# Messages by natural edge tile, and the dispatch placed between the turns of the sums, in a two-layer GNN and mixture-of-experts kernel

## The chip, the cores and the metric

The kernel runs on one core of a Trainium2 chip. The metric is device microseconds of one execution, from the launch to the end on that core. Before the change three runs gave 4209.37, 4212.74 and 4214.22 us; their median, 4212.74 us, is the time before. The five engines are called by the names of the profile: PE (TensorE, with PEld for its weight loads), DVE (VectorE), ACT (ScalarE), POOL (GpSimd) and SP (SyncE, which issues transfers).

## The reference, cut to what matters

There are 6250 nodes of 256 features (49 blocks of 128 nodes), and 100,000 edges, sorted by `dst` and in random order of `src`. Layer 0 is a graph convolution and a mixture of experts, layer 1 a relational convolution and a second mixture:

```python
x = x + _L0_gnn_ref(_layernorm(x), edge_index, edge_weight, W, b, W1, b1, W2, b2)
x = x + _L0_ffn_ref(_layernorm(x)[None], router_w, w1, b1, w2, b2)[0]     # 8 experts, top 2
x = x + _L1_gnn_ref(edge_index, _layernorm(x), edge_type_8, weight, h_bias, loop_weight)
x = x + _L1_ffn_ref(_layernorm(x)[None], ...)[0]                           # 6 experts, top 2
```

The convolution of layer 0 is what the change touches. In it `row` is `src`, `col` is `dst`, and every node has a loop of weight 1:

```python
deg = segment_sum(ew_sl, row_sl)
norm = rsqrt(deg)[row_sl] * ew_sl * rsqrt(deg)[col_sl]
msgs = (h @ W)[col_sl] * norm[:, None]
h7 = segment_sum(msgs, row_sl) + b
out = relu(h7 @ W1 + b1) @ W2 + b2
```

So a row of `dst` is read for each edge, weighted, and summed at `src`. Then each node is normed, its two experts are chosen, and its row is sent to each of them.

## The kernel before, in words

**Keys (to 418 us).** The edges are written to a table in DRAM of 782 tiles of 128 edges (L152 to L189). A check finds whether they are sorted (L206), and a branch (L209) reorders them if not. `tile_list` (L243) then makes a list of tiles by block of `dst`: a tile whose edges lie in two blocks is in the list once for each, so the list has T = 830 entries, padded to TL = 832. The tiles are gathered in the list's order into `M` (L317). `dloc` is an edge's row within the entry's block; an edge of the other block is masked (`mine`, L335). `srcT`, `ewT`, `dlocT` and `idxT` are the transposed columns, one per entry (L352 to L355). From `srcT` come an edge's block by source and its row in it; `eq` (L547) holds 49 masks of 832 columns, from which are counted (`pcnt`, L555) and placed (`ppos`, L603 to L605) all edges in order of their source, and from which the degrees come (L665 to L680, DCH = 32 columns at a time). `at` (L614) is each message's place in `msgs`; a masked edge has the place NOWHERE, past the end.

**Messages (418 to 1505 us, L736 to L773).** `acc` holds the rows of all 49 blocks in SBUF, scaled by `dinv` (L731). For each list entry, one fp32 matmul of a 128x128 selection `sT` (L753, eight entries at a time, from `lane_rows`) with the entry's block of `acc` gives 128 rows (L758; the profile has two records for each such matmul). ACT weights them (L761), and POOL scatters them with one indirect DMA to their places in `msgs` (L764), which checks bounds, so that NOWHERE is skipped. Four buffers of eight entries (`msg`, L754) are in flight. X is loaded and `b2` added on the way (L743 to L751).

**Sums by source (1505 to 2003 us, L777 to L799).** The messages come back in order of source, eight tiles at a time, on SP's and ACT's queues in turn (L783, three buffers). DVE computes `key` (L785) and half of the selections `m` (L787), POOL the other half, each one ahead of its matmul (L795). PE multiplies (L797, into one of four PSUM buffers), and DVE adds to the tile's block of `acc` (L799). Which block that is is read from a register, so the address is known at run time only.

**Dispatch (2003 to 2206 us).** For 13 groups of four blocks, four stages run one behind the other (`in_stages`, L1063, L1071). `hidden0` scales `acc` on ACT (L974), transposes it, and applies Relu. `tokens` multiplies by W2 (L989), adds to X (L992) and takes the norm's statistics (L390 to L401). `choose` norms on ACT (L1003), multiplies with the router (L1009), and picks two experts (`route`, L851, on DVE but for an Exp). `send` counts places (L1028 to L1047) and issues two indirect DMAs per block (L1051). Then the counts of the experts are closed (L1078 to L1138) and the experts' tiles are fetched (L1156).

The weights of layer 0's experts (`fw1`, `fw2`, 2 MB each), their biases and W2 are loaded on SP's queue at the start of the dispatch (L930 to L934). What follows, the experts of layer 0, the products of layer 1 (`hx`), and its sums with layer 1's experts between their turns (`layer1`, L1395), is not changed but for where its memory lies.

**What sets the order.** [...] The framework orders instructions by their place in the program and by when it expects them to be ready, but it does not move one into or out of a branch. Reads and writes of `acc` at run-time addresses count as touching all of it.

Of the kernel before, what the change touches and what calls it, by code (L numbers as in the profile page):

```python
# [32 lines left out]
NOWHERE = 127 + 128 * 1024  # L33
TS = TL + NT
# [5 lines left out]
DCH = 32  # L40
# [12 lines left out]
def gnn_ffn_kernel(ctx: ExitStack, tc: tile.TileContext, a, out):  # L53
# [18 lines left out]
    g0p = graph0.enter_context(tc.tile_pool(name="graph0", bufs=1))  # L72
    loading = ctx.enter_context(ExitStack())
# [203 lines left out]

    turn_i = sp.tile([128, Q * 128], I32, name="turn_i")
    nc.gpsimd.iota(turn_i, pattern=[[1, Q * 128]], base=0, channel_multiplier=0)
    turn = g0p.tile([128, Q * 128], F32, name="turn")  # L280
# [43 lines left out]

    Mf = M.bitcast(F32)
    dloc = sp.tile([128, Q, 128], F32, name="dloc")
    srcm = sp.tile([128, Q, 128], F32, name="srcm")
    idxf = sp.tile([128, Q, 128], F32, name="idxf")
    mine = sp.tile([128, Q, 128], F32, name="mine")
    dlocb = sp.tile([128, Q, 128], BF16, name="dlocb")  # L330
# [3 lines left out]
    nc.scalar.copy(dlocb, dloc)  # L334
    nc.vector.tensor_scalar(mine, dloc, 0.0, None, op0=OP.is_ge)  # L335
    nc.vector.scalar_tensor_tensor(mine, dloc, 128.0, mine, op0=OP.is_lt, op1=OP.mult)
    nc.vector.scalar_tensor_tensor(srcm, M[:, :, :, 1], 1.0, mine, op0=OP.add, op1=OP.mult)
    lane_rows = dram.tile([Q * 128, 128], BF16, name="lane_rows")
    nc.sync.dma_start(lane_rows.rearrange("(q p) e -> p q e", p=128), dlocb)


    def to_edges(name, pool, rows, dt):
        t = pool.tile([128, Q * 128], dt, name=name)
        for q0 in range(0, Q, 4):
            n = min(4, Q - q0)
            pt = psum_mm(f"p_{name}{q0}")
            for q in range(n):
                nc.tensor.transpose(pt[:, q * 128 : (q + 1) * 128], rows(q0 + q), ident)
            nc.scalar.copy(t[:, q0 * 128 : (q0 + n) * 128], pt[:, : n * 128])
        return t  # L350

    srcT = to_edges("srcT", g0p, lambda q: srcm[:, q], F32)  # L352
    ewT = to_edges("ewT", g0p, lambda q: Mf[:, q, :, 2], F32)
    dlocT = to_edges("dlocT", ed, lambda q: dloc[:, q], BF16)
    idxT = to_edges("idxT", ed, lambda q: idxf[:, q], I32)  # L355
# [56 lines left out]
    def transpose_to(name, dest, x, bias=None):  # L412

        pt = p_tr.tile([128, 2, 128], F32, tag="tr", name=f"pt_{name}")
        for k in range(2):
            nc.tensor.transpose(pt[:, k, :], x[:, k * 128 : (k + 1) * 128], ident)  # L416
        if bias is None:
            nc.scalar.copy(dest, pt)
        else:
            for k in range(2):  # L420
                nc.scalar.activation(dest[:, k, :], pt[:, k, :], AF.Identity, bias=bias[k])
# [63 lines left out]
    mv0 = g0p.tile([128, NT, 2], F32, name="mv0")  # L485
# [6 lines left out]
    ve0 = g0p.tile([128, NT], F32, name="ve0")  # L492
    nc.vector.tensor_scalar(ve0, mv0[:, :, 1], EPS, None, op0=OP.add)
    rstd0 = rsqrt("ln0", ve0, [128, NT])
    shift0 = g0p.tile([128, NT], F32, name="shift0")
# [40 lines left out]
    srcT_i = kp.tile([128, TL], I32, name="srcT_i", tag="t1")  # L536
    nc.vector.tensor_scalar(srcT_i, srcT[:, :TL], -1.0, None, op0=OP.add)
    key_i = kp.tile([128, TL], I32, name="key_i", tag="t2")
    nc.vector.tensor_scalar(key_i, srcT_i, 7, None, op0=OP.arith_shift_right)
    hib = kp.tile([128, TL], BF16, name="hib")  # L540
    nc.vector.tensor_copy(hib, key_i)
    nc.vector.tensor_scalar(key_i, srcT_i, 127, None, op0=OP.bitwise_and)
    lob = kp.tile([128, TL], BF16, name="lob")
    nc.vector.tensor_copy(lob, key_i)
    eq = kp.tile([128, NT, TL], BF16, name="eq")
# [7 lines left out]
    for b in range(NT):  # L553
        for h in range(2):
            nc.tensor.matmul(  # L555
                pcnt[h][:NT, :TH],
                sel[:, NT - 1 - b : 2 * NT - 1 - b],
                eq[:, b, h * TH : (h + 1) * TH],
                start=(b == 0),
                stop=(b == NT - 1),  # L560
            )
    cnts = kp.tile([NT, TL], F32, name="cnts", tag="t1")
    for h in range(2):
        nc.scalar.copy(cnts[:, h * TH : (h + 1) * TH], pcnt[h][:NT, :TH])
    base = kp.tile([NT, TL], F32, name="base", tag="t3")
    one = ones[:NT, 0:1].to_broadcast([NT, TL])
    nc.vector.tensor_tensor_scan(base, one, cnts, 0.0, op0=OP.mult, op1=OP.add)
    tots = kp.tile([NT, 1], F32, name="tots")
    nc.vector.tensor_copy(tots, base[:, TL - 1 :])
# [12 lines left out]
    base_i = kp.tile([NT, TL], I32, name="base_i", tag="t2")  # L582
    nc.vector.scalar_tensor_tensor(base_i, base, start0, cnts, op0=OP.add, op1=OP.subtract)
    qr = kp.tile([64 + NT, TL], F16, name="qr")
    nc.vector.memset(qr, 0.0)
    half_i = kp.tile([NT, TL], I32, name="half_i", tag="t4")
# [10 lines left out]
    pos = kp.tile([128, TL], F32, name="pos", tag="t3")  # L597
    nc.vector.memset(pos, float(NOWHERE))
    for b in range(NT):
        for h in range(2):  # L600
            cs = slice(h * TH, (h + 1) * TH)
            pp = psum_mm(f"ppos{b}_{h}")
            nc.tensor.matmul(pp[:, :TH], beforeb, eq[:, b, cs], start=True, stop=False)  # L603
            nc.tensor.matmul(pp[:, :TH], selq[:, b : b + 1].to_broadcast([64 + NT, 128]), qr[:, cs], start=False, stop=True)
            nc.vector.copy_predicated(pos[:, cs], eq[:, b, cs].bitcast(U16), pp[:, :TH])  # L605
        next(xws, None)

    place = kp.tile([128, TL], I32, name="place", tag="t1")
    nc.vector.tensor_copy(place, pos)
    slot = kp.tile([128, TL], I32, name="slot", tag="t2")  # L610
    nc.vector.tensor_scalar(slot, place, 7, None, op0=OP.arith_shift_right)
    nc.vector.tensor_scalar(place, place, 127, None, op0=OP.bitwise_and)
    at = g0p.tile([128, TL], I32, name="at")
# [3 lines left out]
    past_s = kp.tile([NT, TL], F32, name="past_s", tag="t4")  # L617
# [8 lines left out]
    lasts = g0p.tile([1, 56], I32, name="lasts")  # L626
    nc.vector.memset(lasts, TS - 1)
    nc.vector.tensor_scalar(lasts[:, :NT], plast[:1, :NT], -1.0, None, op0=OP.add)
    for b0 in range(0, NT, 8):
        slots = blocks_of(lasts, b0, [ENG.SP], TS - 1)  # L630
        for b in range(min(8, NT - b0)):
            ins = nc.sync.dma_start(by_tile[:, bass.ds(slots[b], 1), :], none[:, 0:1, :])
            tc.declare_no_dep(ins.ins, group="tails", reason="every block has a last tile of its own")
            tc.add_to_no_dep_group("tails", ins.ins)
    blks = g0p.tile([1, TL], I32, name="blks")
    firsts = g0p.tile([128, TL], F32, name="firsts")
    first_of = g0p.tile([NT, 128], F32, name="first_of")
# [12 lines left out]
    parts = kp.tile([128, 3, TL], BF16, name="parts")  # L650
    rest = kp.tile([128, TL], F32, name="rest", tag="t1")
    nc.vector.tensor_copy(parts[:, 0], ewT[:, :TL])
    nc.vector.tensor_sub(rest, ewT[:, :TL], parts[:, 0])
# [8 lines left out]
    for c0 in range(0, TL, DCH):  # L662
# [16 lines left out]
        for c in range(DCH):  # L679
# [5 lines left out]
                stop=(c0 + c == TL - 1),  # L685
# [24 lines left out]
    expand = ctx.enter_context(ExitStack())  # L710
    xp = expand.enter_context(tc.tile_pool(name="expand", bufs=3))

    def lanes_of(t0):

        rows = xp.tile([128, 8, 128], BF16, name=f"rows{t0}", tag="rows")
        nc.sync.dma_start(
            rows,
            lane_rows[t0 : t0 + 8, :].rearrange("(o t) e -> o t e", o=1).to_broadcast([128, 8, 128]),
        )
        return rows  # L720

    ahead = [lanes_of(t0) for t0 in (0, 8, 16)]
# [11 lines left out]


    for t0 in range(0, TL, 8):  # L736
        blocks = blocks_of(blkd, t0, [ENG.PE], NT)
        n = min(8, T - t0)
        rows = ahead.pop(0)
        if t0 + 24 < TL:  # L740
            ahead.append(lanes_of(t0 + 24))

        if t0 % 80 == 40 and t0 // 80 < 4:  # L743
            t = t0 // 80 * 12
            nc.sync.dma_start(X[:, t : t + 12, :], xv[:, t : t + 12, :])
        if t0 == 400:
            nc.sync.dma_start(X[:last, NT - 1, :], a["x"][(NT - 1) * 128 :, :])
        if t0 >= 440 and t0 % 8 == 0 and (t0 - 440) // 8 * 2 < NT:
            t = (t0 - 440) // 8 * 2
            k = min(2, NT - t)  # L750
# [751 lines left out]
```

## Time and profile before

| | us |
|---|---|
| median of three runs (4209.37 to 4214.22) | 4212.74 |
| the profiled execution | 4220.04 |
| its span, first to last instruction | 4218.3 |
| PE busy, share of the span | 3288.1 (78%) |
| POOL busy | 2307.8 (55%) |
| DVE busy | 2072.4 (49%) |
| ACT busy | 1168.6 (28%) |

Around the span lie 1.7 us. The stages of the span are: keys 418, messages 1087, sums by source 498, dispatch 203, experts of layer 0 270, products of layer 1 479, layer 1's sums and experts 1263. In rows of groups, the first number after the bar is the group's busy time in us, the second the mean ns of one instruction; behind the next bar stands the engine's idle time just ahead of them, and what ended most of it. In rows of a timeline, the first two numbers are the start and the duration in us, and the brackets hold the idle time ahead of it and its releaser. "issue" as a releaser means that nothing in the profile was waited for.

### The profile page before, as it was taken

Reading aid. Unit: us, or ns where it says so; the run is one execution under the profiler, and the core shown is the slowest. Engines: PE = TensorE matmul, PEld = TensorE weight load, DVE = VectorE, ACT = ScalarE, POOL = GpSimd, SP = SyncE. Lnnn points to the kernel's source line nnn. Section 1 sums busy time; section 2 is a strip of 40 time slices with the busy share of each in tenths; the row PEclk is TensorE's granted clock in tenths of the full one; section 3 lists DMA queues with packets and bytes.
Section 4 is the critical chain, followed back from the end, with each engine's and each line's share of the span. In section 5 each row is a group of like instructions: output and inputs, shape, how many; then the busy total and the mean of one; then the engine's idle time right before and its main releaser. Section 6 shows DMA issues by size and latency. Waiting matters only on the chain.

```text
span 4218.3 us, 49934 instructions
## 1 busy us (share of the span) xinstructions
PE 3288.1 (78%) x13207; PEld 2125.4 (50%) x13207; DVE 2072.4 (49%) x5527; ACT 1168.6 (28%) x2569; POOL 2307.8 (55%) x2488
## 2 busy tenths in 40 slices
PE   2886555565555559999749977999679999999999
PEld 1565444444444335554537743444256666666656
DVE  5676200000000058888563357665456666666652
ACT  3312433333333300000434433665012222222213
POOL 1000777777777755555470048333767777777750
PEclk9998877767777779999769988999589999999999
DMA  4413433333333356666333335444655555555540
GB/s 169 155 43 110 153 124 121 123 123 120 121 122 122 108 190 230 225 227 209 106 115 107 109 105 201 194 194 205 190 142 151 152 151 153 150 155 150 146 117 9
DMA packets 235392, 611.60 MB, mean 145 GB/s; under 512 B 44269, under 2 KB 128482, under 8 KB 215139
## 3 DMA queue, kind: packets, MB, share of 16 engines
q0 software_dynamic: 102928, 294.81, 22.5%
q1 hardware_dynamic: 105200, 234.80, 16.6%
q10 hardware_dynamic: 26976, 78.69, 5.4%
q8 instruction: 115, 1.88, 0.2%
q14 instruction: 173, 1.42, 0.1%
HBM read 371.46 MB, written 243.18 MB: 146 GB/s over the span
## 4 chain that ended last, share of the span: by engine, by line
PE 42%; DVE 10%; POOL 4%; issue 3%; DMA 3%; ACT 2%; DVEq 1%; SPq 0%; POOLq 0%; ACTq 0%
PE ph_e1a L428 6%; PE py1a L904 6%; PE pa1a L823 5%; PE pa L797 5%; PE ph_e2a L428 5%; PE phx L1265 4%; DVE acc L799 3%; PE pf L1184 2%; PE pf L1200 2%; POOL m L795 2%; DVE rest L1275 1%; PE pg L989 1%; DVE acc L827 1%; PE pt_fh L416 1%; DVE hx L1259 1%
## 5 line engine op out<-in xcount | busy, mean ns | idle before, releaser
L764 POOL DMA_INDIRECT msgs<-msg,at x830 | 833.1, 1004 | 599.2 <-ACT msg L761 388.6
L815 POOL DMA_INDIRECT g1a<-hx,idxT x830 | 826.6, 996 | 321.1 <-PE pa1a L823 148.0
L758 PE MATMUL px<-acc,sT 128*128 x1660 | 601.4, 541 | 481.7 <-ACT msg L761 447.6
L758 PEld LDWEIGHTS px<-acc,sT 128*128 128x128 f32 x1660 | 459.3, 284 | 623.1 <-ACT msg L761 487.6
L761 ACT ACTIVATE msg<-px,ewT 128x256 f32<-128x256 f32 x830 | 356.7, 474 | 697.1 <-DMA msgs<-msg,at 568.6
L827 DVE TENSOR_TENSOR acc<-acc,pa1a 128x256 f32 x830 | 346.6, 418 | 341.7 <-PE pa1a L823 311.1
L797 PE MATMUL pa<-g,m 128*128 128x256 f32 x1660 | 448.2, 419 | 84.5 <-DVE m L787 44.7
L823 PE MATMUL pa1a<-g1a,m1a 128*128 128x256 bf16 x2490 | 376.4, 283 | 51.9 <-DMA g1a<-hx,idxT 37.2
L1265 PE MATMUL phx<-wr,xT 128*128 128x512 f32 x784 | 371.7, 618 | 29.2 <-DVE rest L1275 22.8
L797 PEld LDWEIGHTS pa<-g,m 128*128 128x128 f32 x1660 | 249.5, 189 | 283.5 <-issue 114.8
L795 POOL TENSOR_SCALAR m<-lanes,key 128x128 f32<-128x128 f32 x414 | 263.2, 651 | 229.0 <-PE pa L797 206.4
L799 DVE TENSOR_TENSOR acc<-acc,pa 128x256 f32 x830 | 348.2, 419 | 73.6 <-PE pa L797 6.0
L823 PEld LDWEIGHTS <-m1a 128*128 128x128 bf16 x2490 | 243.2, 100 | 277.3 <-issue 191.7
L755 DVE COPY msg<-srcT 128x32 f32<-128x32 f32 x104 | 18.8, 182 | 700.2 <-DMA msgs<-msg,at 700.0
L904 PE MATMUL py1a<-w_L_ffn_expert_w,v2a 128*128 128x256 f32 x1176 | 286.6, 384 | 6.0 <-DVE acc L827 3.0
L428 PE MATMUL ph_e1a<-xT3a,w_L_ffn_expert_w 128*128 128x512 f32 (+2 forms) x672 | 288.0, 555 | 0.0
L428 PE MATMUL ph_e2a<-v1a,w_L_ffn_expert_w 128*128 128x512 f32 (+2 forms) x672 | 280.1, 542 | 2.1 <-DVE acc L827 1.3
L1225 POOL DMA_INDIRECT y<-ys,ats x98 | 98.0, 1000 | 298.3 <-DMA ys<-fy 272.5
L435 ACT ACTIVATE v1a<-ph_e1a,cols 128x512 f32<-128x512 f32 (+2 forms) x168 | 106.5, 634 | 538.7 <-PE ph_e1a L428 538.6
L1265 PEld LDWEIGHTS phx<-wr,xT 128*128 128x128 f32 x784 | 149.1, 198 | 189.6 <-issue 163.4
L904 PEld LDWEIGHTS py1a<-w_L_ffn_expert_w,v2a 128*128 128x128 f32 x1176 | 208.8, 190 | 44.2 <-ACT v2a L435 10.1
L753 DVE TENSOR_SCALAR sT<-rows,part 128x1024 f32<-128x1024 bf16 x104 | 83.8, 808 | 236.0 <-PE px L758 233.5
(610 smaller groups left out, 4285.6 us busy)
## 6 DMA issues: line engine op xcount, KB each, us to landing
hx<-hx SPq DMA_DIRECT2D x49, 1536.0 KB, 5.0
g<-msgs SPq DMA_DIRECT2D x52, 1040.0 KB
g<-msgs ACTq DMA_DIRECT2D x52, 1040.0 KB, 4.9
rows<-lane_rows SPq DMA_DIRECT2D x104, 256.0 KB, 3.6
fx<-xs SPq DMA_DIRECT2D x105, 128.0 KB, 2.0
ys<-fy ACTq DMA_DIRECT2D x105, 128.0 KB
msgs<-msg,at POOLq DMA_INDIRECT x830
g1a<-hx,idxT POOLq DMA_INDIRECT x830
```

What stands on the lines that cost most here:

```text
L428: nc.tensor.matmul(ps[:, :ncols], w[:, k, f * 128 : (f + 1) * 128], xT[:, k, :ncols], start=(k == 0), stop=(k == 1),)
L758: nc.tensor.matmul(ps[:, :D], sT[:, j, :], acc[:, bass.ds(blocks[j] * D, D)], start=True, stop=True)
L761: nc.scalar.activation(msg[:, j, :D], ps[:, :D], AF.Copy, scale=ewT[:, t0 + j : t0 + j + 1])
L764: ins = nc.gpsimd.indirect_dma_start(out=msgs, out_offset=bass.IndirectOffsetOnAxis(ap=at[:, t0 + j : t0 + j + 1], axis=0), in_=msg[:, j, ...
L795: nc.gpsimd.tensor_scalar(m[:, j], lanes, key[:, j : j + 1], None, op0=OP.is_equal)
L797: nc.tensor.matmul(ps[:, :D], m[:, j, :], g[:, j, :D], start=True, stop=True)
L799: nc.vector.tensor_add(here, here, ps[:, :D])
L815: nc.gpsimd.indirect_dma_start(out=g, out_offset=None, in_=table, in_offset=bass.IndirectOffsetOnAxis(ap=idxT[:, t0 + j : t0 + j + 1], axi ...
L823: nc.tensor.matmul(ps[:, :D], m[:, j, :], g[:, k * D : (k + 1) * D], start=(k == 0), stop=(k == 2))
L827: nc.vector.tensor_add(here, here, ps[:, :D])
L904: nc.tensor.matmul(ps[:, :D], hT[:, k, j : j + 128], w[:, k, :], start=(k == 0), stop=(k == 1))
L1265: nc.tensor.matmul(ps, xT[:, k, :], wr[:, k, r : r + 2, :].rearrange("p r o -> p (r o)"), start=(k == 0), stop=(k == 1),)
```

## The change

The message stage no longer follows the list by block of `dst`. It takes the 782 natural tiles, in their order in the table (read back as `Mn`). A tile begins in some block `blkn`; its edges lie in that block or in the next. Each tile has two selections, and two matmuls that accumulate. If an edge of some tile lay further off (`nfar`), another branch gathers the rows of `dst` by indirect DMA instead. All edges are real but for the padding, which goes to a spare row of `msgs`, so the scatter is not checked. The columns of the keys are TN = 784 rather than 832, and DCH is 28.

The sums become a generator that yields after each add, as the sums of layer 1 do, and its loads are all on SP. The dispatch becomes one generator per group (`send_group`), of which one step is taken per turn: five steps for the scaled and transposed rows, an empty one, four for W2 and the statistics, one for the norm, six for the normed rows and the router, then three for choice and counts, one for places, and one for each block's two token DMAs. A group begins when the turn is past 16.46 turns per block plus 12. Whether every block's last tile lies before that is counted on the device (`nlate_s`); if not, a branch runs the sums and then the dispatch. `fw2` and its bias are loaded after the dispatch, `fw1` and W2 ahead of the sums.

The diff, cut to its core:

```diff
+TN = (C_ + 7) // 8 * 8
+QN = (C_ + 127) // 128
+NH = TN // 2
+TS = TL + NT + 1
+S_TURNS, S_SLACK = C_ / NT + 0.5, 12
-DCH = 32
+DCH = 28
...
+    Mn = sp.tile([128, QN, 128, 4], I32, name="Mn")
+    nc.sync.dma_start(
+        Mn[:, : QN - 1].rearrange("p q e r -> p q (e r)"), table[:whole].rearrange("(q p) x -> p q x", p=128)
+    )
...
+    real = sp.tile([128, QN, 128], F32, name="real")
+    nc.vector.tensor_scalar(real, Mn[:, :, :, 0], float(NP), None, op0=OP.is_lt)
+    nc.vector.scalar_tensor_tensor(srcm, Mn[:, :, :, 1], 1.0, real, op0=OP.add, op1=OP.mult)
+    for q in range(QN):
+        nc.vector.tensor_scalar(lane[:, q], Mn[:, q, :, 0], firstn[:, q : q + 1], None, op0=OP.subtract)
...
-    nc.scalar.copy(dlocb, dloc)
-    nc.vector.tensor_scalar(mine, dloc, 0.0, None, op0=OP.is_ge)
-    nc.vector.scalar_tensor_tensor(mine, dloc, 128.0, mine, op0=OP.is_lt, op1=OP.mult)
...
-    eq = kp.tile([128, NT, TL], BF16, name="eq")
+    eq = kp.tile([128, NT, TN], BF16, name="eq")
...
+    nc.vector.tensor_scalar(late_s, part[:NT], S_TURNS, S_TURNS + S_SLACK, op0=OP.mult, op1=OP.add)
+    nc.vector.tensor_tensor(late_s, tend_s, late_s, OP.is_gt)
...
+    def messages(tag, near):
+            for t0 in range(0, TN, 8):
+                n = min(8, C_ - t0)
...
+                    blocks = blocks_of(blkn, t0, [ENG.PE], NT - 1)
+                    sT = xp.tile([128, 2, 8, 128], F32, name=f"sT{tag}{t0}", tag="sT", bufs=2)
+                    for k in range(2):
+                        nc.vector.tensor_scalar(
+                            sT[:, k], rows, far_parts[:, k : k + 1], None, op0=OP.is_equal
+                        )
...
+                        if j % 2 == 0:
+                            pair = psum_mm(f"px{tag}{t0 + j}")
+                        come = pair[:, j % 2 * D : (j % 2 + 1) * D]
+                        for k in range(2):
+                            nc.tensor.matmul(
+                                come,
+                                sT[:, k, j, :],
+                                acc[:, bass.ds(blocks[j] * D + k * D, D)],
+                                start=(k == 0),
+                                stop=(k == 1),
+                            )
...
                     ins = nc.gpsimd.indirect_dma_start(
                         out=msgs,
                         out_offset=bass.IndirectOffsetOnAxis(ap=at[:, t0 + j : t0 + j + 1], axis=0),
                         in_=msg[:, j, :],
                         in_offset=None,
-                        bounds_check=128 * TS - 1,
-                        oob_is_err=False,
                     )
...
+    with tc.If(nfar_v > 0) as far_cmp:
+        messages("f", False)
+    with far_cmp.Else():
+        messages("n", True)
...
+    def sum_messages(pool, tag):
-            eng = nc.sync if t0 % 16 else nc.scalar
-            eng.dma_start(g, by_tile[:, t0 : t0 + 8, :])
+            nc.sync.dma_start(g, by_tile[:, t0 : t0 + 8, :])
-            m = mp.tile([128, 8, 128], F32, name=f"m0_{t0}", tag="m")
+            m = pool.tile([128, 8, 128], F32, name=f"m0{tag}_{t0}", tag="m", bufs=2)
...
             for j in range(n):
                 if j >= 4:
                     nc.gpsimd.tensor_scalar(m[:, j], lanes, key[:, j : j + 1], None, op0=OP.is_equal)
+            for j in range(n):
...
                 nc.vector.tensor_add(here, here, ps[:, :D])
+                yield t0 + j + 1
...
+    def send_group(g, n, mlp, tag, seen):
+        for i in range(n + 1):
+            if i < n:
+                h7 = work.tile([128, D], F32, name=f"h7{tag}_{g + i}", tag="xn", bufs=3)
+                nc.scalar.activation(
+                    h7, acc[:, (g + i) * D : (g + i + 1) * D], AF.Copy, scale=dinv[:, g + i : g + i + 1]
+                )
+                rows.append(h7)
+            if i:
+                transpose_to(
+                    f"h7{tag}_{g + i - 1}",
+                    uT[:, :, (i - 1) * 128 : i * 128],
+                    rows[i - 1],
+                    [b_mlp[:, k : k + 1] for k in range(2)],
+                )
+            yield
+        yield
...
+            nc.vector.tensor_add(X[:, t, :], X[:, t, :], ps[:, :D])
+            nc.vector.bn_stats(st, X[:, t, :])
+            nc.vector.bn_aggr(mv[:, i, :], st)
+            yield
...
+        oh1, oh2, wa, wb = yield from route(f"0{tag}_{g}", mlp, L, n, 8, False)
...
+    def sum_and_send(tag, early):
+            def step(through):
+                nonlocal steps
+                if steps is None and waiting and through(sum(waiting[0])):
+                    g, n = waiting.pop(0)
+                    steps = send_group(g, n, mlp, tag, seen)
+                if steps is not None and next(steps, steps) is steps:
+                    steps = None
+            for turn in sum_messages(sump, tag):
+                if early:
+                    step(lambda blocks: S_TURNS * blocks + S_SLACK <= turn)
+            while steps is not None or waiting:
+                step(lambda blocks: True)
...
+    with tc.If(nlate_sv > 0) as late_s_cmp:
+        sum_and_send("l", False)
+    with late_s_cmp.Else():
+        sum_and_send("e", True)
+    fp2 = ffn0.enter_context(tc.tile_pool(name="ffn0b", bufs=1, side="right"))
+    fw2 = load_experts(fp2, "L0_ffn_w2").rearrange("p e k f -> p (e k f)")
+    fb2 = rows_of("L0_ffn_b2", fp2)
...
-    in_stages([hidden0, tokens, choose, send], GROUPS)
```

## The prediction

> **What bounds the kernel now.** I read the stretches first, cut where the last instruction of one stage meets the first of the next: keys to 418 us, messages to 1505, sums by source to 2003, dispatch to 2206. Each row holds the length, each engine's busy us (instructions), TensorE's clock and the DMA.
> ```profile
> core 0: us, PE busy (x) PEld busy (x) DVE busy (x) ACT busy (x) POOL busy (x), PEclk, DMA share, GB/s
> 0.00:418.00 418.00, 265.88 (x1515) 193.26 (x1516) 284.44 (x527) 119.88 (x279) 15.14 (x22) 0.91 0.36 117
> 418.00:1505.00 1087.00, 599.82 (x1659) 457.96 (x1657) 112.94 (x226) 356.19 (x829) 833.15 (x830) 0.74 0.38 124
> 1505.00:2003.00 498.00, 448.16 (x1660) 249.49 (x1660) 414.69 (x1040) 0.00 (x0) 263.15 (x414) 0.99 0.66 223
> 2003.00:2206.00 203.00, 127.30 (x627) 100.91 (x627) 127.34 (x826) 85.14 (x213) 122.88 (x147) 0.71 0.29 102
> ```
> The message stage is POOL's: 833 busy of 1087, and POOL's timeline shows the rest as a fixed 0.30 us between issues. The first two rows are checked scatters of messages, the last two unchecked gathers of layer 1.
> ```profile
> 1459.30 0.98 POOL L764 DMA_INDIRECT msgs<-msg,at  x1 [0.30 <-issue]
> 1460.59 0.98 POOL L764 DMA_INDIRECT msgs<-msg,at  x1 [0.30 <-DMA msgs<-msg,at]
> ...
> 3199.89 0.95 POOL L815 DMA_INDIRECT g1a<-hx,idxT  x1 [0.30 <-issue]
> 3201.14 0.95 POOL L815 DMA_INDIRECT g1a<-hx,idxT  x1 [0.30 <-PE pa1a L823]
> ```
> A period of 1.289 us checked, 1.249 unchecked. The sums stage is different: DVE's timeline repeats every 4.63 us (1698.44 to 1703.08), eight tiles each.
> ```profile
> 1698.44 0.16 DVE L785 TENSOR_TENSOR key<-g,firsts 128x8 f32<-128x8 f32 x1
> 1698.63 0.42 DVE L799 TENSOR_TENSOR acc<-acc,pa 128x256 f32 x1
> 1698.96 0.71 DVE L787 TENSOR_TENSOR m<-lanes,key 128x512 f32<-128x512 f32 x1
> 1699.60 3.56 DVE L799 TENSOR_TENSOR acc<-acc,pa 128x256 f32 x7
> 1703.08 0.16 DVE L785 TENSOR_TENSOR key<-g,firsts 128x8 f32<-128x8 f32 x1
> ```
> Seven adds in 3.56 us are 0.525 apart at 0.42 each; an add followed by something that doesn't touch acc is 0.33 apart. DVE is full, but 0.1 us in each add's wake is a gap that a small independent operation can use. PE is nearly as full: 16 matmul records in 4.28 of the 4.63 us, 0.267 each.
> ```profile
> L758 PE MATMUL px<-acc,sT 128*128 x1660 | 601.4, 541 | 481.7 <-ACT msg L761 447.6 <-DMA X<-in_x 30.1 <-DVE sT L753 4.0
> L753 DVE TENSOR_SCALAR sT<-rows,part 128x1024 f32<-128x1024 bf16 x104 | 83.8, 808 | 236.0 <-PE px L758 233.5 <-DMA rows<-lane_rows 2.5
> L795 POOL TENSOR_SCALAR m<-lanes,key 128x128 f32<-128x128 f32 x414 | 263.2, 651 | 229.0 <-PE pa L797 206.4 <-DVE key L785 20.2 <-DVE acc L799 2.4
> L1051 POOL DMA_INDIRECT xs<-tok,ats x98 | 96.3, 982 | 38.3 <-issue 23.1 <-DVE mv L401 5.2 <-DVE r L392 4.7
> L673 DVE TENSOR_TENSOR we<-parts,eq 128x1568 bf16<-128x1568 bf16 x78 | 71.3, 966 | 0.0
> L665 DVE TENSOR_TENSOR ohl<-lob,lanes_b 128x4096 bf16<-128x4096 bf16 x26 | 59.3, 2281 | 3.8 <-PE pdeg L680 3.8
> ```
>
> [...] message buffers come back much later than 0.98 us, and the DMA share is only 0.38, so the stage is issue, not bandwidth. [...] the 137 message issues that overlap an sT average 1.098 us, the others 0.985. [...] the sequencer records at L206 and L209 have 0.04 to 0.23, and a register load ahead of it of 0.5 to 0.67.
>
> **The change, part by part** (us against the profiled execution: 4220.0, span 4218.3).
>
> *Messages.* 830 issues become 782, one for each natural tile of edges (100,000 / 128). Today 830 x 1.289 = 1070, plus 137 x 0.113 = 15.5 of interference, 0.149 for each of 104 sT: 1085.5, and the stage measures 1085.9. Afterwards each group of eight has two sT: 196 x 0.149 = 29. What an unchecked scatter costs isn't shown; it lies between 1.289 (the check is free) and 1.249 (like the unchecked gather); nothing suggests a check makes an issue shorter. I take 1.269: 782 x 1.269 + 29 = 1021, **-65** (-80 to -49). PE doubles to four records a tile, 4 x 0.267 = 1.07, under POOL's 1.27; ACT's 0.47 and DVE's 1.8 per group of eight are covered too. If PE stayed at clock 0.74 its 1.07 would be 1.45 and set the stage (rival).
>
> *Keys.* L547, L605, L665 and L673 (203 us of DVE) and pcnt, ppos and pdeg (209 of PE) scale with 832 columns, now 784: -5.8% is 12 us on either. srcT no longer waits for the gathered M (ready at 84.6), so the keys may start up to 15 earlier; DVE's loads and stats of x, to 118, stay, so I count 3. Mn's load and its masks replace mine and dlocb in idle DVE time. **-15** (-28 to 0).
>
> *Three seams.* What stands inside a branch is issued after it. (a) Into the messages: the first rows loads and sT, at 386 to 392 today under the scaling of acc (396 to 416), come after a register load and branch: landing 3.6, sT 2 x 0.8, first matmuls, less the 2 us that the first message takes today: **+5** (0 to 10). (b) Into the sums: a branch, and fw1, fb1 and W2 now ahead of the first g on SP's queue (3.3 MB, 15 us at 223 GB/s if nothing of it gets out earlier); SP is idle at the end of the messages, so **+4** (0 to 15). (c) fw2 and fb2 (3 MB, 14 us) load after the dispatch, ahead of the fx loads, under the counting chain: **+5** (0 to 14). g moves wholly to SP: 0.33 of issue per 4.63 us is nothing.
>
> *Dispatch between the turns.* This is where I chose. Counted on the reference's edges, the tiles by source end 8.9 turns or more inside the bound, so the interleaved branch runs. The 203 us go; what they held comes back in the sums as X us per group of four tiles (12.25 groups), plus a last group of one tile behind the last turn (13 dependent steps, about 14) and token landings, counting and the first fx (10). Per group: PE, 4 x 4 records of 0.267 for pg2 (4.3), pl and transposes (about 4.6), so 8.9. DVE, 12 operations of 0.42 and 0.17 (4.0), about 50 small ones spaced 0.2 (the root alone runs 2030.34 to 2032.95), and a wait: ACT's h7 reads acc, the next add writes acc at an address known only at run time, so that add must wait 0.50 plus two handovers, 0.55 lost four times (2.2); behind it stand all of DVE's queue, then PSUM's four buffers, then PE. If everything small falls into gaps, DVE's 37.05 us for 64 turns become some 45 and PE's 34.2 become 43: X = 8. If the engines only take turns, each step costs what its busiest engine needs: h7 2.1 (the waits), pg2 4.1 (PE), root 2.6 (DVE), logits 2.0 (PE, less its lead), route and places 6.4 (DVE): X = 17. POOL: eight token issues of 1.28 within four turns (10.2 us) stand ahead of the next m (L795: POOL ends at 1701.31, PE starts on it at 1704.79, a lead of 3.5; POOL is also idle 2.1 in 4.63): 0 to 4.6 of the wait come through. I take 13: 498 + 12.25 x 13 + 24 = 681 against 498 + 203 = 701, **-20** (X = 8: -81; X = 22: +90). The 17.4 us that PE waits for W2 at 2023 today are within the 203.
>
> Sum: -65 - 15 + 5 + 4 + 5 - 20 = **-86**: 4134 beside 4220.0. The profiled execution is 7.3 above the median of 4212.74; the same difference gives 4127.
>
> **Rivals.** *Slower: the turns serialize.* DVE and PE are both full in the sums, nothing has room, and the token issues hold up POOL's m: X = 17 + 4.6 = 22, +90 in place of -20, 4237. It decides from X = 20, where the rest's -66 is used up. For it: [...] alone the dispatch needs only 12 us a group. Against: layer 1 interleaves the same way and keeps PE busy for 99% from 3150 to 3780 (its add there follows the gathers, not DVE's own pace). *PE takes over the messages*: at clock 0.74, 782 x 1.45 = 1134, +48 in place of -65, 4240. [...] *Near-perfect overlap*: X = 8, unchecked at 1.249, keys -25: -81 - 80 - 25 + 14 = -172, 4041. *It doesn't do what it says*: the late branch runs, dispatch stays behind: -66, 4147; against it is the count of tiles.
>
> **How the numbers follow.** Forecast (X 10 to 20, 4090 to 4210) 0.55, of which 0.03 lies within 0.2% of before; overlap (4020 to 4090) 0.18; turns serialize 0.15; PE 0.06; late branch 0.03; something unseen and slower 0.03. 0.2% (8 us) is about what a measurement of this kernel can tell from no change. So faster 0.52 + 0.18 + 0.03 = 0.73, same 0.03, slower 0.24. The range leaves out half of the overlap case (0.09) and half of the slow ones (0.11): 4045 to 4240.
>
> **What would show it.** Messages: POOL's period between 1.249 and 1.289, about 1020 us from first to last issue, PE's clock above 0.85. Keys: first message issue near 408. Sums: adds up to 1.1 us apart where an h7 reads acc, 26 thick turns and 38 of 0.58 us per group, some 660 us with POOL never the releaser of a matmul for more than 5 us. I'd be wrong if PE waits on POOL m after each burst of tokens, or if DVE, not POOL, sets the messages.

## The result, and the profile after

| | before | after |
|---|---|---|
| median of eight runs, us | 4212.82 (4209.37 to 4214.99) | 4225.27 (4220.61 to 4228.4) |
| span of the profiled execution | 4218.3 | 4226.6 |

The ratio of the times is 1.0027 (95% interval 1.0016 to 1.0037): slower by 12 us, where 86 less were forecast. The stages, cut at the same events in every trace (first and last issue of messages, first and last record of PE in the sums, last token, first fx):

| us | before | after | e1 | e2 | e11 |
|---|---|---|---|---|---|
| keys, to the first message | 418.2 | 402.3 | 401.0 | 401.4 | 405.2 |
| messages | 1085.9 | 1023.8 | 1023.1 | 1023.7 | 1025.4 |
| end of messages to first sum | 10.1 | 20.1 | 19.8 | 20.4 | 11.0 |
| sums, first to last | 487.9 | 733.1 | 666.8 | 493.4 | 486.1 |
| last sum to last token | 201.2 | 24.3 | 22.5 | 226.3 | 196.4 |
| last token to first fx | 2.0 | 6.0 | 6.6 | 6.2 | 2.0 |
| the rest | 2013.0 | 2017.0 | 2010.9 | 2014.3 | 2011.6 |

(e1, e2 and e11 are experiments below, on chips where the kernel before takes 4212.66 to 4216.51.) Keys and messages gave back 78, near the 75 forecast. From the end of the messages to the first fx it was 701.2 and is now 783.5: 82 are lost, where 11 should have been gained. (The rest, which ranges from 2010.9 to 2017.0 in the table, adds 4 here, so that the two spans differ by 8.3.) The stretches of the kernel after, with the columns of those of before:
```profile
402.30:1426.00 1023.70, 786.45 (x3118) 610.22 (x3117) 164.69 (x311) 369.24 (x781) 785.84 (x782) 0.91 0.39 131
1426.00:1446.10 20.10, 0.00 (x0) 0.00 (x0) 1.77 (x12) 0.00 (x0) 0.74 (x2) 0.50 0.80 275
1446.10:2179.20 733.10, 580.51 (x2234) 382.81 (x2234) 496.87 (x1755) 91.96 (x246) 353.13 (x502) 0.90 0.49 165
```
In the messages PE's clock rose from 0.74 to 0.91, and POOL still sets the pace: the timeline shows a period of 1.27 with the same 0.30 between issues (its median over the stage is 1.276, before 1.289).
```profile
1423.81 0.97 POOL L858 DMA_INDIRECT msgs<-msgn,at  x1 [0.30 <-issue]
1425.08 0.97 POOL L858 DMA_INDIRECT msgs<-msgn,at  x1 [0.30 <-issue]
```
In the sums no engine is full: PE is busy for 580.5 of 733.1 and DVE for 496.9. The groups name the waits. PE's records stood behind adds for 5.8 us in the kernel before (the first row), and now for 79.2; DVE's adds stand behind h7 and PE for 41 each:
```profile
L797 PE MATMUL pa<-g,m 128*128 128x256 f32 x1660 | 448.2, 419 | 84.5 <-DVE m L787 44.7 <-POOL m L795 33.3 <-DVE acc L799 5.8
L895 PE MATMUL pa0e<-g0e,m0e 128*128 128x256 f32 x1660 | 502.1, 440 | 186.2 <-DVE acc L897 79.2 <-DVE m0e L884 40.6 <-POOL m0e L892 37.4
L897 DVE TENSOR_TENSOR acc<-acc,pa0e 128x256 f32 x830 | 347.4, 419 | 126.9 <-ACT h7e L1072 41.6 <-PE pa0e L895 41.1 <-DVE acc L897 6.4
```
The larger part is lost before any step of the dispatch has begun. The first group starts at turn 78; the 78 turns ahead of it take 96.7 us by the starts of their adds, where 78 x 4.63 / 8 = 45.1 are due. DVE's timeline there repeats every 10.3 us:
```profile
1483.09 0.69 DVE L884 TENSOR_TENSOR m0e<-lanes,keye 128x512 f32<-128x512 f32 x1 [1.83 <-PE pa0e L895]
1483.70 0.87 DVE L897 TENSOR_TENSOR acc<-acc,pa0e 128x256 f32 x2
1488.01 0.17 DVE L882 TENSOR_TENSOR keye<-g0e,firsts 128x8 f32<-128x8 f32 x1 [3.44 <-DMA g0e<-msgs]
1488.16 0.42 DVE L897 TENSOR_TENSOR acc<-acc,pa0e 128x256 f32 x1
1489.09 2.52 DVE L897 TENSOR_TENSOR acc<-acc,pa0e 128x256 f32 x5 [0.51 <-DVE acc L897]
1493.45 0.69 DVE L884 TENSOR_TENSOR m0e<-lanes,keye 128x512 f32<-128x512 f32 x1 [1.83 <-PE pa0e L895]
```
Of the eight tiles that come with one g I speak as a block here. The key at 1488.01 belongs to a block whose first add comes at 1509.50, 17 adds later. Its g was issued at 1483.09, when PE had read the last tile of the block three before (g has three buffers), and took 4.9 to land. No add behind the key in DVE's queue passed it: DVE stood for 3.44, and PE, which needed those adds to free one of PSUM's four buffers, stood for 3.32 until the add at 1488.16:
```profile
1488.64 5.22 PE L895 MATMUL pa0e<-g0e,m0e 128*128 128x256 f32 x12 [3.32 <-DVE acc L897]
```
In the kernel before, keys stand nine adds ahead from the fifth block on. A g issued as late (1693.01 for the key at 1698.44) has landed when its key's turn comes, and the same stretch has no gap. In the changed kernel's trace keys stand 17 ahead in nearly all blocks from the fourth to the twentieth, and from the twenty-third on between 6 and 14. The waits (engine, line, what it waited for: us in total, times, longest), in the first row of the kernel before in its sums from 1515 us on, in the others of the kernel after between 1446 and 1640 us:
```profile
DVE key L785 <- DMA g<-msgs: 1.3, 1, 1.3
PE pa0e L895 <- DVE acc L897: 58.0, 37, 3.7
DVE keye L882 <- DMA g0e<-msgs: 53.6, 18, 3.8
```

### The profile page after: what moved, and what is told of

The parts are those of the page before. It is cut to its first block, busy times and chain, and to the rows that moved or that the text cites. A ratio compares the mean times of both kernels' runs of the same rounds, so it can differ in the third digit from the quotient of the medians.

```text
span 4226.6 us, 52427 instructions
## 1 busy us (share of the span) xinstructions
PE 3488.2 (83%) x14645; PEld 2318.7 (55%) x14645; DVE 2093.3 (50%) x5670; ACT 1194.2 (28%) x2567; POOL 2266.0 (54%) x2440
## 3 DMA queue, kind: packets, MB, share of 16 engines
q1 hardware_dynamic: 112636, 290.21, 20.4%
## 4 chain that ended last, share of the span: by engine, by line
PE 38%; DVE 9%; issue 4%; DMA 2%; ACT 2%; POOL 2%; DVEq 0%; ACTq 0%; POOLq 0%; SPq 0%
PE ph_e1a L473 6%; PE py1a L1001 5%; PE pa1a L922 5%; PE ph_e2a L473 5%; PE phx L1415 4%; PE pf L1334 2%; PE pf L1350 2%; PE pa0e L895 2%; DVE rest L1425 1%; DVE acc L897 1%; DVE acc L926 1%; PE pt_fh L461 1%; DMA g1a<-hx,idxT 1%; DVE hx L1409 1%; PE pcb1a L1517 1%
## 5 line engine op out<-in xcount | busy, mean ns | idle before, releaser
L858 POOL DMA_INDIRECT msgs<-msgn,at x782 | 785.9, 1005 | 550.7 <-DMA rowsn<-lane_rows 312.9
L840 PE MATMUL pxn<-acc,sTn 128*128 x3128 | 790.8, 413 | 243.1 <-DVE sTn L821 216.2
L840 PEld LDWEIGHTS pxn<-acc,sTn 128*128 128x128 f32 x3128 | 613.5, 206 | 420.3 <-DVE sTn L821 282.4
L895 PE MATMUL pa0e<-g0e,m0e 128*128 128x256 f32 x1660 | 502.1, 440 | 186.2 <-DVE acc L897 79.2
L855 ACT ACTIVATE msgn<-pxn,ewT 128x256 f32<-128x256 f32 x782 | 370.0, 473 | 638.4 <-PE pxn L840 451.0
L895 PEld LDWEIGHTS pa0e<-g0e,m0e 128*128 128x128 f32 x1660 | 298.2, 209 | 355.9 <-DVE acc L897 136.2
L892 POOL TENSOR_SCALAR m0e<-lanes,keye 128x128 f32<-128x128 f32 x414 | 265.9, 657 | 346.9 <-PE pa0e L895 274.7
L831 DVE COPY msgn<-srcT 128x32 f32<-128x32 f32 x98 | 18.0, 186 | 830.2 <-DMA msgs<-msgn,at 748.1
L897 DVE TENSOR_TENSOR acc<-acc,pa0e 128x256 f32 x830 | 347.4, 419 | 126.9 <-ACT h7e L1072 41.6
L1001 PEld LDWEIGHTS py1a<-w_L_ffn_expert_w,v2a 128*128 128x128 f32 x1176 | 208.6, 190 | 44.4 <-ACT v2a L480 10.2
L1002 DVE SCALAR_TENSOR_TENSOR X<-py1a,C1a,X 128x256 f32<-128x256 f32 x294 | 139.0, 481 | 112.3 <-PE py1a L1001 111.3
```

What stands on the lines that cost most here:

```text
L840: nc.tensor.matmul(come, sT[:, k, j, :], acc[:, bass.ds(blocks[j] * D + k * D, D)], start=(k == 0), stop=(k == 1),)
L855: nc.scalar.activation(msg[:, j, :D], come, AF.Copy, scale=ewT[:, t0 + j : t0 + j + 1])
L858: ins = nc.gpsimd.indirect_dma_start(out=msgs, out_offset=bass.IndirectOffsetOnAxis(ap=at[:, t0 + j : t0 + j + 1], axis=0), in_=msg[:, j, ...
L892: nc.gpsimd.tensor_scalar(m[:, j], lanes, key[:, j : j + 1], None, op0=OP.is_equal)
L895: nc.tensor.matmul(ps[:, :D], m[:, j, :], g[:, j, :D], start=True, stop=True)
L897: nc.vector.tensor_add(here, here, ps[:, :D])
```

## The experiments

e1 to e4, and e11 and e12, ran on chips on which the kernel before takes 4212.66 and 4216.51 us. e5 to e10 ran on another chip, on which it takes 4535.94 (e5 to e7) and 4531.3 (e8 to e10); the stages of indirect transfers are longer there (messages 1162 for 1023 in the same kernel), the sums are not (665.8 in e10, 666.8 in e1). So these six are compared with each other, by stage and by ratio to the kernel before.

**e1: the key's place.** One edge of issue order for each block from the third:
```diff
-            nc.vector.tensor_sub(key[:, :n], g[:, :n, D], firsts[:, t0 : t0 + n])
+            ins = nc.vector.tensor_sub(key[:, :n], g[:, :n, D], firsts[:, t0 : t0 + n])
+            if t0 >= 10:
+                tc.add_manual_dep(
+                    ins.ins,
+                    adds[t0 - 10].name,
+                    mybir.DependencyInfo(mybir.DependencyClass.NoSync, mybir.DependencyReason.DATA),
+                    reason="key",
+                )
...
+                adds.append(nc.vector.tensor_add(here, here, ps[:, :D]).ins)
```


> The changed kernel, with one edge more in DVE's order: the key of a block of eight tiles is issued behind the add nine tiles ahead of the block, as in the kernel before; nothing else differs. Theory A (order of DVE's queue): in the first twenty blocks of the changed kernel the key stands 17 adds ahead of its block and waits there for its transfer, with the adds that free the transfer's buffer behind it; the first 78 turns take 96.7 us there where 45.1 are due, and the 64 turns of the first group 83.4 where the other groups take 50.5. Both go: -84, a time of 4141 (4130 to 4165), no wait of DVE on g over 1 us between 1450 and 1650. Theory B (the turns serialize, 19 us a group, and the slow start is the weights' transfers or a cold clock): the time stays within 10 of 4225.

4153.43 us (4150.4 to 4155.05), 0.9861 (0.9845 to 0.9877) of before: 72 less than the changed kernel. DVE's timeline at the same place, and its waits on g over the whole of the sums:
```profile
1483.17 0.16 DVE L883 TENSOR_TENSOR keye<-g0e,firsts 128x8 f32<-128x8 f32 x1
1483.36 0.42 DVE L905 TENSOR_TENSOR acc<-acc,pa0e 128x256 f32 x1
1483.69 0.71 DVE L892 TENSOR_TENSOR m0e<-lanes,keye 128x512 f32<-128x512 f32 x1
1484.39 3.57 DVE L905 TENSOR_TENSOR acc<-acc,pa0e 128x256 f32 x7
1487.88 0.16 DVE L883 TENSOR_TENSOR keye<-g0e,firsts 128x8 f32<-128x8 f32 x1
```
```profile
DVE keye L883 <- DMA g0e<-msgs: 2.8, 2, 2.6
```
The period is 4.7 again, and between 1450 and 1650 us DVE waits 0.2 for g; the wait of 2.6 comes later. Theory A holds. The sums fell by 66.3, not the 84 of theory A: the first group still takes 59.1 for 64 turns, and the later ones 51.6 on the mean where they took 50.5.

**e3: the same order put into the kernel before.** Loads and keys are traced three blocks ahead (`bring` issues both, the key in program order), and the last add of a block behind the key:
```diff
+        coming = [bring(t0) for t0 in (0, 8, 16)]
...
+                if j == n - 1 and t0 + 24 < TL:
+                    coming.append(bring(t0 + 24))
                 here = acc[:, bass.ds(blocks[j] * D, D)]
-                nc.vector.tensor_add(here, here, ps[:, :D])
+                add = nc.vector.tensor_add(here, here, ps[:, :D])
+                if j == n - 1 and t0 + 24 < TL:
+                    tc.keep_in_program_order(add)
```


> The kernel before, with its load and key of each block traced three blocks ahead, so that on DVE's queue the key stands 17 adds ahead of its block's first add, in all blocks from the fourth; the same instructions otherwise. Theory A: each of 101 blocks then takes 9 to 10.3 us in place of 4.63, since the transfer of 4.9 us lies open; +440 to +570, a time of 4650 to 4790, with some 3.4 us of DVE waiting on g in every block. Theory B (weights or clock make the slow start): as before within 20, since no weights are loaded there.

4772.59 us, 1.1331 (1.1308 to 1.1354): +560, all of it in the sums (1046.8 for 487.9). In its timeline a key comes every 10.2 us behind a gap of some 5.1, and the waits count 101 of them:
```profile
1811.42 0.17 DVE L786 TENSOR_TENSOR key<-g,firsts 128x8 f32<-128x8 f32 x1 [5.18 <-DMA g<-msgs]
1821.62 0.17 DVE L786 TENSOR_TENSOR key<-g,firsts 128x8 f32<-128x8 f32 x1 [5.10 <-DMA g<-msgs]
```
```profile
DVE key L786 <- DMA g<-msgs: 515.4, 101, 5.5
```
So the order alone makes the loss, without branch, weights or interleaving.

**e12: the unmended order without the interleaving**, and **e2: the mended order without it.** Both make the sums in the branch and the groups behind them:
```diff
-        sum_and_send("e", True)
+        sum_and_send("e", False)
```


> e2 without the edge that pins the keys: the sums stand in their branch alone, no step of the dispatch between them, and DVE's order is the one the framework gives. Its program has the key 17 adds ahead in blocks 3 to 16. Theory A (the order comes with the sums as the branch has them, not with the interleaved steps): these 14 blocks take some 10 us in place of 4.63, sums 493 + 14 x 5.6 = 570. Theory B (the slow start needs the interleaved steps): 493.

> As e1, and the branch that runs makes all sums first and the groups of the dispatch behind them, one step after the other, as the late branch does. Keys -16, messages -62 and the seam into the sums +19 stay, sums 498 as before; the groups now run one behind the other and not in four stages, so the dispatch is longer than the 203 of before. Theory A (the interleaving costs 13.5 us a group once DVE's order is right): e1 is faster than this kernel by 14 or more. Theory B (19 us a group or more): this kernel is faster than e1, by up to 54.

e12: 4264.08 (1.0112; 1.0096 to 1.0127), sums 571.0, as theory A has it, with the wait on g in full though no step lies between the turns:
```profile
DVE keye L882 <- DMA g0e<-msgs: 48.6, 15, 3.7
```
e2: 4187.95 (0.9944; 0.9928 to 0.996), 34.5 over e1, sums 493.4. So the bad order comes with the sums as they are rewritten and stand in the branch, not with the interleaved steps, and interleaving does beat the same steps one after the other. It is another question whether it beats the pipeline of before, which e11 asks.

**e11: the message half alone.** Sums, loads of weights and the dispatch in four stages are those of the kernel before, word for word, behind the new messages.

> The message half of the change alone: natural tiles, two selections, unchecked scatter, 784 columns of keys; sums, dispatch and loads of weights are those of the kernel before, word for word, in four stages behind the sums. Keys -16 and messages -62 stay; the seam into the sums is that of before (10), sums and dispatch the 691 of before: -78 to -73, 0.981 to 0.983 of the kernel before where the messages are at one per 1.31. Theory A (the interleaving, even with DVE's order mended, only gives what it takes: e1 needs 696 from the first sum to the first fx, before 691): this kernel is faster than e1 by 10 to 20 us, 0.003 to 0.005 of the ratio. Theory B (the interleaving gains and only the order hid it): it is slower than e1 (0.986 to 0.988).

4138.96 (4133.84 to 4142.68), 0.9817 (0.9803 to 0.983): faster than e1 (0.9861) by the ratio, each on its own chip. From the end of the messages to the first fx it needs 695.5, e1 715.7. The old pipeline overlaps the four stages with each other for 196.4; the new groups, run alone (e2), take 226.3. A part of what the interleaving gains replaces what the stages had gained already.

**e4: the check put back** on the message issues.
```diff
                         in_=msg[:, j, :],
                         in_offset=None,
+                        bounds_check=128 * TS - 1,
+                        oob_is_err=False,
```


> The changed kernel with the bounds check put back on the 782 message issues; no place lies past the bound, so all are still written. If the check costs what the medians of the two periods show (1.289 checked before, 1.276 unchecked after): 782 x 0.013 = +10, a time of 4235, with a period of 1.289. If the difference of the periods comes from something else (the two matmuls, the places all being real): no change, 4225.

4231.06 (1.0045; 1.003 to 1.0059). The interval overlaps that of the changed kernel, so the total doesn't decide; the trace does: the median period is 1.289, and the stage takes 1031.3, 7.5 more. The check costs 0.013 us an issue (e1, on the same chip as e4, has 1.276 too).

**e5: the tokens one by one.** In e1 POOL issues eight in a row, and its next m for the sums comes after them:
```profile
1751.69 1.06 POOL L1178 DMA_INDIRECT xs<-toke,ats  x1 [1.05 <-issue]
...
1760.68 0.98 POOL L1178 DMA_INDIRECT xs<-toke,ats  x1 [0.30 <-issue]
1761.68 7.18 POOL L900 TENSOR_SCALAR m0e<-lanes,keye 128x128 f32<-128x128 f32 x12
```
```profile
1763.63 0.42 DVE L905 TENSOR_TENSOR acc<-acc,pa0e 128x256 f32 x1 [4.69 <-PE pa0e L903]
```
```profile
PE pa0e L903 <- POOL m0e L900: 57.2, 19, 7.8
```
The edit, on top of e1's, puts a group's eight into a list, and every eighth turn sends one, behind POOL's m of that turn:
```diff
-            yield
             for at in (at1, at2):
-                ins = nc.gpsimd.indirect_dma_start(
+                outbox.append((now_at[0] + 24, tok[:, i, :], at[:, t : t + 1]))
+        yield
...
+                if turn % 8 == 0 and outbox and outbox[0][0] <= turn:
+                    send(tag, *outbox.pop(0)[1:])
```


> As e1, and the eight token issues of a group leave one at a time, every eighth turn, each behind POOL's m of that turn's block, in place of eight in a row (10.2 us). In e1 a row is followed by one gap of 4.4 to 7.6 us between adds, and PE waits 57.2 us in 19 waits for POOL's m. Theory A (what the tokens hold up comes through): these gaps go, -45 to -60, and two or three issues more stand behind the last turn, +3: a time of 4105 (4095 to 4118). Theory B (the gaps only move to DVE and PE, which are as full): within 12 of 4153.

0.9763 (0.9744 to 0.9782) of before on its chip. Its sums take 609.9, those of e1 there (e10) 665.8: -55.9, as theory A has it. But the last token to the first fx rose from 6.9 to 27.0. POOL's and DVE's timelines there:
```profile
2214.04 26.25 POOL L1346 TENSOR_SCALAR X<-X,stretch,offset 128x256 f32<-128x256 f32 x49
```
```profile
2215.37 0.15 DVE L1294 CAST tails<-pta 1x8 int32<-1x8 f32 x1 [1.17 <-issue]
2215.45 24.37 DVE L1291 TENSOR_SCALAR places<-first 1x112 int32<-1x112 f32 x1
```
A DVE operation on 112 elements is recorded as 24.37 us, and ends 0.5 us before POOL's row of 49 scalings does; SP waits for the places before it may issue fx.

**e8: e5 with the scalings later.**
```diff
-    nc.vector.tensor_scalar(ats, to, float(TE * 128 - 1), None, op0=OP.min)
+    tc.keep_in_program_order(nc.vector.tensor_scalar(ats, to, float(TE * 128 - 1), None, op0=OP.min))
+    stretch2 = const.tile([128, NT], F32, name="stretch2")
+    tc.keep_in_program_order(nc.vector.tensor_copy(stretch2, stretch))
```


> As e5, and POOL's 49 scalings of X read a copy of stretch that DVE makes after the last of its counting steps, so that they can't begin before the places are counted. In e5 they ran from 2214.0 to 2240.3 without a pause, and a DVE operation of one partition by 112 elements that began at 2215.4 is recorded as 24.4 us long; the time from the last token to the first fx was 27.0. Theory A (POOL's row of scalings keeps that DVE operation from its turn): no such operation lasts over 1 us ahead of the first fx, and that time falls to some 7. Theory B (the places wait for something else, such as the landing of tokens): it stays near 27.

0.9723 (0.9708 to 0.9738); the last token to the first fx 7.3. The row now starts behind the copy, as long as before, and what PE waits for m in the sums is down from 52.3 (e10; 57.2 in e1) to 8.4:
```profile
2231.60 26.27 POOL L1348 TENSOR_SCALAR X<-X,stretch,offset 128x256 f32<-128x256 f32 x49 [14.20 <-DVE stretch L1319]
```
```profile
PE pa0e L905 <- POOL m0e L902: 8.4, 18, 1.0
```

**e6: the seams.** fw1 and fb1 on ACT's queue, the tokens in the tails' group:
```diff
-    fw1 = load_experts(fp, "L0_ffn_w1").rearrange("p e k f -> p (e k f)")
+    fw1 = load_experts(fp, "L0_ffn_w1", nc.scalar).rearrange("p e k f -> p (e k f)")
...
-                tc.add_to_no_dep_group(f"tokens{tag}", ins.ins)
+                tc.add_to_no_dep_group("tokens", ins.ins)
```


> As e1, with two edits at the seams: fw1 and fb1 are loaded on ACT's queue in place of SP's, and the token issues are put in the group of transfers in which the zero tails of the experts stand, so that the tails don't wait for them. Theory A: the first g no longer stands behind nine loads and their transfers, and the 19.8 us from the end of the messages to PE's first record of the sums become the 10 of the kernel before; the time from the last token to the first fx falls from 6.6 to 2 or 3; together -14, a time of 4139. Theory B (the seam is the landing of the last scattered messages, and the tail is the landing of the last tokens): both stay, 4153.

0.9885 (0.9867 to 0.9904), no better than e10 (0.9876). The seam into the sums fell from 21.5 (e10) to 14.2: 7.3 less, where theory A has 10. The tail grew from 6.9 to 14.2, against both theories: four of fw1's loads and fb1 were put behind the branch, and the operation that makes the places is 12.12 us long here. So e6 doesn't say what holds the tail.

**e7: h7 on DVE.**
```diff
-                nc.scalar.activation(
-                    h7, acc[:, (g + i) * D : (g + i + 1) * D], AF.Copy, scale=dinv[:, g + i : g + i + 1]
+                nc.vector.tensor_scalar(
+                    h7, acc[:, (g + i) * D : (g + i + 1) * D], dinv[:, g + i : g + i + 1], None, op0=OP.mult
                 )
```


> As e1, with h7 (the scaled row of acc) made by DVE in place of ACT, so that no add waits for another engine's read of acc. In e1 DVE's adds wait 48.7 us in 41 waits for h7. Theory A (these waits stand on the path, as 0.55 four times a group and more): they go, and 49 operations of some 0.3 us come onto DVE: -20 to -35, a time of 4118 to 4133. Theory B (PE or POOL is as late at those turns): within 10 of 4153.

0.9839 (0.9822 to 0.9856), sums 650.8 for e10's 665.8: -15, between the theories. The 49 operations add 20.8 us of busy time to DVE. If all of that is on the path, some 36 of e1's 48.7 us of waits were on it too; this is an estimate.

**e10** is e1 again, and **e9** joins e8 with e7, the tails' group, and fw1 loaded inside the sums.

> e1 once more, word for word, on the chip of e8 and e9, so that these can be compared with it: 0.986 of the kernel before.

> e8, with h7 on DVE, the tokens in the group of the tails, and fw1 loaded inside the sums, one expert's part behind each block's g, so that nothing stands ahead of the first g but W2. Against e1 on the same chip, by stage: seam into the sums 20 to 10 (-10), sums -55 for the tokens and -10 to -15 for h7, last token to fx 6.6 to 3 (-4), two tokens more at the end (+3): -76 to -81, of 4153 about 0.981 to 0.982 of e1's time. If the gains share a cause (DVE full at 0.525 an add whatever goes): -55 to -60, 0.986.

e10: 0.9876 (0.9861 to 0.9891). e9: 4384.84 us beside 4531.3, 0.9675 (0.9662 to 0.9688): the lowest ratio here, 4384.84 / 4477.28 = 0.979 of e10. By stage against e10: seam 13.2 for 21.5, sums 604.0 for 665.8, last token to fx 7.2 for 6.9. The two profiled executions differ by 82.3, and 11.1 of these lie behind the first fx: in e10 a DVE operation beside POOL's row of scalings is recorded as 24.1 us there. e8, with that row later, has 20.2 less than e10 behind the first fx, so not all of e8's and e9's lead over e10 belongs to the sums. Beside the spread tokens h7 on DVE brings only 4 (604.0 for e8's 608.2), and the tail doesn't depend on the tokens' group.

## Why the prediction was wrong

**The step that failed** is the first term of "498 + 12.25 x 13 + 24 = 681": 498 takes a turn of the sums at 4.63 us per eight, as in the kernel before, for every turn that holds no step. I took that for a property of the engines. It is one of DVE's issue order as well, which the framework makes anew when the sums are rewritten. The turns ahead of the first group ran at 10.3 per eight (51.6 lost), and the first group's 64 took 83.4 where later ones take 50.5 (32.9 lost). e1 takes 66.3 of these 84.5 away, e3 makes the loss in the kernel before, e12 shows it without the interleaving. With the order mended the change saves 59.2 us (e1), of the 86 forecast; what is still missing is mostly X and the seam into the sums. What in the rewritten sums led the framework to that order stays open: sums outside a branch have the good order with the same messages (e11), but the branch, the two buffers of m, POOL's m traced ahead of all of a block's matmuls, and the one queue for g were not tried apart.

**Messages**: 1021 forecast, 1023.8 measured; period 1.276 between the two bounds; PE stayed under POOL, with 786.45 / 782 = 1.01 us of busy time a tile at a clock of 0.91. The rival in which PE takes them over is out. What raised the clock from 0.74 isn't shown.

**Keys and the seam into the messages**: -10 forecast, -15.9 measured.

**The seam into the sums**: +4 forecast, +10 measured. SP held nine loads, W2 and zeros from 1427.97 on, and issued the first g at 1440.18; with fw1 moved the seam is 14.2 (e6) and 13.2 (e9). Of the rest, some 6 us lie between the zeros (1433.87) and the first g, and e6 has as much there (1565.68 to 1571.70); no run explains them. "SP is idle at the end of the messages" was right and of no use: SP stood at the first of the loads until the last message had landed, so none was early. That their memory is what the messages free is the likely reason; it wasn't tried.

**The last group, counting and the first fx**: 14 for the last group, 10 for landings, counting and the first fx, and 5 for fw2, 29 in all; measured 30.3. The sum is luck. The last group took 24.3 to its last token, with ten token issues in a row on POOL (2190.93 to 2203.47), and from there to the first fx it was 6.0, not 15.

**X**: 13 forecast; 50.5 - 37.0 = 13.5 in the changed kernel's later groups, (666.8 - 487.9) / 12 = 14.9 in e1. Of the 14.9, 55.9 / 12 = 4.7 are the tokens ahead of m: the upper end of the 0 to 4.6 that I had bounded, while my 13 names no share for them. The h7 waits are by the estimate above some 36 / 12 = 3, for 2.2 (and e7 gets 15 / 12 = 1.2 of it). So the size was near, and at that size the gain was nearly nothing from the start: e1 needs 715.7 from messages to fx, the old pipeline 695.5. Only with the tokens spread (655.9 in e8, on the other chip, where e10 needs 716.7) does the interleaving gain on it.

**The slower rival** came near in its number (4237) and not in its cause: X would have been 22. One part of it was true. The sign that I had named, PE waiting more than 5 us for POOL's m behind a burst of tokens, is there: 5.95 and 5.14 at the longest in the changed kernel, 7.8 in e1. It costs the 4.7 of X above, and not the order's 84.5.

## What to carry to other kernels

When a loop is rewritten, look at where each engine's queue puts an operation that waits for a transfer, and which work behind it frees that transfer's buffer: one key eight places too early doubled the period (10.3 us for 4.63). An interleaving has to be priced against the overlap that it takes apart, not against an idle engine. A burst on a queue that also feeds the loop was paid nearly in full here (55.9 of sums for 57.2 of waits), and spreading it was a small edit.

## What the runs showed of the hardware

A VectorE TENSOR_SCALAR is recorded as 12.12 (e6), 24.37 (e5) and 24.1 us (e7 and e10) beside a row of 49 GpSimd instructions of some 0.54 each. With the row moved behind it, no such record is left (e8 and e9). By what means the row does this isn't shown. All four cases are on the slower chip. In the changed kernel's own profile three operations of the same line as in e7 and e10 (there L1291, here L1283) began 0.1, 0.3 and 1.4 us behind the start of the same row, and took 0.27, 0.41 and 0.27. What decides between the long records and the short ones isn't shown, nor whether e5's tail of 27.0 would come on the other chips.

The check of an indirect scatter costs 0.013 us of an issue's 1.289 (e4). In the kernel before, ACT, released by the transfers, writes a message buffer again at 1007.25, 1.65 us behind the recorded end of the last of that buffer's eight issues (1004.62, 0.98 long); the median over the stage is 1.66. And two chips differ by 7.6% on the kernel before, while the sums of e1 and e10 differ by 0.2%: on the slower one POOL's median period in the messages is the same 1.276, but 108 of its gaps between issues are over 0.6 us and up to 3.2, together 173 (e10), and in e1 none is over 0.31. What makes them isn't shown.
